# Four equal routing parts with one indirect zeroing transfer in the first expert layer, and re-dealt routing pieces ahead of the second

## The chip, the cores and the metric

The kernel runs on one core of a Trainium2 chip. The metric is the device time of one execution in microseconds (us). The engines are named as in the profile: PE (TensorE, the matrix unit; PEld is its weight load), DVE (VectorE), ACT (ScalarE), POOL (GpSimd) and SP (SyncE, which here only issues transfers). Each engine works through its own instructions in order and waits on semaphores for the others. A transfer is issued by SP, by ACT's queue or, where its addresses are computed row by row, by POOL as an indirect transfer. PSUM is the accumulator memory that PE writes into, in banks.

## The reference

The input is 2048 tokens (8 sequences of 256) of width 128, float32. Six residual steps follow one another:

```python
x = x + 0.5 * moe(layernorm(x))       # routed experts, first layer
x = x + attention(layernorm(x))       # 16 heads of width 8
x = x + 0.5 * moe(layernorm(x))       # the same weights, second layer
x = x + 0.5 * channel_mix(layernorm(x))
x = x + gated_conv(layernorm(x))      # a long convolution by Fourier transform
x = x + 0.5 * channel_mix(layernorm(x))

def moe(s):                           # 8 experts, each token goes to 2
    h = rmsnorm(s @ W_in.T, in_norm_w)
    logits = h @ Wr.T
    idx = top_k(logits + expert_bias, 2)
    g = softmax(logits at idx)
    for e in range(8):                # d_ff = 512
        oe = rmsnorm((silu(h @ Wg[e].T) * (h @ Wu[e].T)) @ Wd[e].T, enorm_w[e])
        out += (gate of e, 0 where it was not chosen) * oe
    return rmsnorm(out, out_norm_w) @ W_out.T
```

The kernel multiplies only the rows that were routed to an expert, so it has to sort 4096 (token, choice) rows by expert on the chip.

## The kernel before

**Layout.** The 2048 tokens are 16 tiles of 128, held in four chunks `xs[0..3]` of four tiles. The program order on PE, DVE, ACT and SP is written out by hand: whatever piece of the program is called first stands first in each engine's queue. POOL's routing transfers keep their program order too.

**Routing, `dispatch(f, i, parts, mp)`.** Layer `f` (0 or 1) is routed in parts; `parts[i]` names the first tile and the number of tiles. `EARLY` (L48) has five parts for layer one (2, 2, 4, 4 and 4 tiles), `LATE` (L49) five for layer two (4, 4, 4, 2, 2). A part is a list of pieces, called in this order, with the lines at which their instructions show in the profile:

- `turned`: PE transposes the tiles into the bank `pxt` (L337), ACT copies them out as `xnt` (L339).
- `product` twice, two tiles each: PE multiplies by the folded weights `win_r` (L359), ACT copies the result to `u` (L363) and sums its squares (L367).
- `measured`: DVE takes the mean and variance of the tiles (L347 to L351). Because of the layer norm the root of the mean square is corrected with `z`.
- `normed`: DVE forms `ri`, ACT takes its root (L377), DVE its reciprocal (L378). In the paced parts of layer two POOL takes the power instead.
- `logits` (DVE, L385) and `scaled` (ACT, L390), which writes the normalised rows into `hrow`, once for each of the two choices, with the token's number in column 128. A row has `ROW` = 129 words.
- `choice(0)` and `choice(1)` (DVE, L397 to L411): the best and the second best expert as one-hot vectors, and `mask`, their sum.
- `places`: the position of every row inside its expert's region. A triangular matrix `tri` times `mask` counts the earlier tokens of the tile (L418), one product with `ones` for each tile but the last adds the earlier tiles of the part (L420), one more product adds the earlier parts from `macc` (L427), and DVE extends `macc` by the part's counts `cnt` (L431, L432). DVE then forms `both`, `lsel`, `at_row`, `pos` and the integers `posi` (L434 to L445).
- `rows`: POOL writes each tile's 128 rows to their positions in the DRAM array `hs`, one indirect transfer for each tile and choice (L452), 32 in a layer.

`stagger(chunks, 4)` interleaves the parts of layer one: piece s - 4c of part c is called in step s, so a part starts four pieces after the one before it.

**The table.** Each expert has a region of `hs`. The experts read it in blocks of 256 or 128 rows whose last ones reach past the expert's count, so in layer one `zeros(first)` (L546) first writes 256 zero rows behind each expert's last row. It stands in `table` (L467), after the counts `pcnt` (L474), and `first` holds the eight start rows. Its core:

```python
for e in range(E):
    queue = (nc.sync, nc.scalar)[e % 2]
    row = nc.values_load(first[0:1, e : e + 1], engines=[queue.engine], ...)
    ins = queue.dma_start(hss[0][bass.ds(row, TT), :]..., zero)       # L553
```

The rest of `table` is a chain of small DVE operations (L476 to L543) that says for each block which expert it is and where it starts. For layer two the regions are cleared in advance, during the first expert stage, by `clear_rows` (`hs<-blank`, issued by SP).

**The experts.** `experts` takes 21 blocks in a fixed order (more if the table asks for them). SP reads an entry of the table into a register, fetches an expert's weights `w_f` (832 KB, L593) and a block of rows `hst_f` (L599); the first three blocks' fetches come ahead of everything, weights first in layer one, rows first in layer two. PE transposes the rows (`pht_f`, L605), multiplies gate and up (`pg_f`, `pu_f`, L615) and down (`py_f`, L638), and POOL scatters the results (L658).

**Around it.** The start of the program loads `x` and the constants, and folds the weights: DVE subtracts the mean (L294 to L298), PE transposes into `pwr` (L300), ACT copies it to `win_r` (L302). The fold stands ahead of all routing. `heads` (L810) holds the attention buffers; `qks[0]` and `qks[1]` are its 128 x 4096 word query and key buffers, first written during the expert stage.

**Layer two's routing** runs inside attention. Attention works in 34 numbered steps with places "a" and "b"; `at(step, place, *pieces)` hangs pieces there. Parts 0, 1 and 2 of `LATE` are spread over steps 12 to 33, and parts 3 and 4 stand in steps 32 to 34 with the end of the last sequence: `turn_back(7)`, `turn_heads(7)` and `out_heads(7)` turn the last averages `po` (L1014) into `x` (banks `pot`, `pcc`, `pwo`, and the addition L934). `keep_warm(out, n)` issues products of 128 columns whose result nobody reads. `root_table` makes ACT load the table of its root function ahead of need.

## Time and profile before

| what | value |
|---|---|
| median of 3 runs | 624.25 us (623.07, 624.25, 624.63) |
| profiled execution | 626.05 us, span 624.1 us, mean granted clock of PE 0.969 |
| busy over the span | PE 522.8 us (84%), DVE 356.1, ACT 271.0, POOL 192.1 |

Busy time of each engine by stretch of the span, in us, with the clock that PE was granted:

| stretch | what runs | PE | DVE | ACT | POOL | clock |
|---|---|---|---|---|---|---|
| 0 to 16.5 | loads, weight fold, first part's routing | 7.0 | 6.8 | 5.7 | 0.8 | 1.00 |
| 16.5 to 64.6 | routing of layer one, to POOL's last row | 16.3 | 27.5 | 18.8 | 30.9 | 1.00 |
| 64.6 to 75.4 | end of the table, first fetches | 0.7 | 3.1 | 0.0 | 0.0 | 1.00 |
| 75.4 to 185.6 | experts of layer one | 105.9 | 53.8 | 32.7 | 49.7 | 1.00 |
| 185.6 to 380.8 | combination, attention, most of layer two's routing | 177.9 | 133.6 | 112.5 | 38.2 | 0.99 |
| 380.8 to 411.8 | last of attention, rest of layer two's routing | 20.4 | 19.1 | 9.7 | 14.4 | 0.62 |
| 411.8 to 521.0 | experts of layer two | 103.1 | 43.8 | 30.5 | 35.4 | 0.98 |
| 521.0 to 624.1 | channel mixes and convolution | 91.5 | 68.6 | 61.0 | 22.7 | 0.96 |

Lines of the timeline read so: start in the span (us), duration (us), engine, line of the program, operation, output <- inputs, number of instructions drawn together, and in brackets how long the engine was idle before it and what ended that. SPq, ACTq and POOLq are those engines' transfer issues. The digits of the page's second part are tenths of busy time in 40 slices of 15.6 us each, and for PEclk tenths of full clock.

### The profile page before, as it was taken

What the parts mean: (1) busy time and instruction counts of PE and PEld (TensorE: products, weight loads), DVE (VectorE), ACT (ScalarE), POOL (GpSimd) and SP (SyncE); (2) the same over time, 40 slices, a digit from 0 to 9 for tenths busy, and PEclk for the clock granted to TensorE, in tenths of its full rate; (3) what the DMA queues carried; (4) which work ended last, traced back from release to release, by engine and by line L of the source; (5) the groups of instructions that cost most, each with busy time, mean ns of one, the idle gap of its engine ahead of it and who ended that gap; (6) DMA issues with size and microseconds to landing.
All of it is one profiled execution on the core that took longest, in us unless ns stands there. A gap on an engine that the chain in (4) does not pass through costs nothing.

```text
span 624.1 us, 11214 instructions
## 1 busy us (share of the span) xinstructions
PE 522.8 (84%) x3879; PEld 399.4 (64%) x3879; DVE 356.1 (57%) x1108; ACT 271.0 (43%) x662; POOL 192.1 (31%) x199
## 2 busy tenths in 40 slices
PE   4531299999989999899899987669999999889996
PEld 3521188898965555556556644449999984558884
DVE  3665255554443566767876884734444442777675
ACT  3532032222332455666765564213233232876265
POOL 0567135743343121001100446402333335520110
PEclk9999999999999999999999996599999998979999
DMA  6112647767723036408111001065778745000002
GB/s 224 35 38 94 202 154 211 207 194 219 218 79 102 27 43 174 168 35 257 51 49 22 26 26 51 31 217 178 216 222 252 216 137 147 1 0 2 2 1 67
DMA packets 38122, 71.70 MB, mean 115 GB/s; under 512 B 4587, under 2 KB 27922, under 8 KB 36912
## 3 DMA queue, kind: packets, MB, share of 16 engines
q1 hardware_dynamic: 33136, 61.97, 33.3%
q0 software_dynamic: 4352, 8.47, 3.9%
q8 instruction: 32, 0.52, 0.3%
q10 hardware_dynamic: 576, 0.53, 0.2%
q14 instruction: 26, 0.21, 0.1%
HBM read 50.10 MB, written 21.38 MB: 115 GB/s over the span
## 4 chain that ended last, share of the span: by engine, by line
PE 45%; ACT 9%; DVE 7%; DMA 5%; issue 3%; SPq 1%; POOL 0%; DVEq 0%; ACTq 0%; POOLq 0%
PE ps L967 8%; PE py_f L638 4%; PE pg_f L615 4%; PE pu_f L615 4%; ACT es L1004 4%; PE po L1014 4%; DMA y<-yrow_f,idx_f 3%; PE pvf L1343 2%; PE pgo L1370 2%; PE pm L950 1%; PE pk_m L1287 1%; DVE m L987 1%; PE pkv_m L1269 1%; PE pr_m L1269 1%; DMA w_f<-in_wall_dram 1%
## 5 line engine op out<-in xcount | busy, mean ns | idle before, releaser
L658 POOL DMA_INDIRECT y<-yrow_f,idx_f x72 | 70.7, 982 | 121.2 <-issue 61.8
L1004 ACT ACTIVATE es<-ps 128x1024 f32<-128x1024 f32 x64 | 65.3, 1020 | 51.7 <-PE ps L967 29.9
L987 DVE TENSOR_REDUCE m<-pm 128x4 f32<-128x1024 f32 x64 | 77.5, 1220 | 13.2 <-PE pm L950 13.1
L967 PE MATMUL ps<-qa,qk 32*128 32x256 f32 x512 | 72.8, 401 | 12.5 <-ACT es L1004 9.6
L452 POOL DMA_INDIRECT hs<-hrow,posi_f x64 | 61.7, 964 | 64.1 <-issue 28.7
L615 PE MATMUL pg_f<-ht_f,w_f 128*128 128x256 f32 (+1 forms) x336 | 71.5, 357 | 3.4 <-DMA w_f<-in_wall_dram 2.8
L638 PE MATMUL py_f<-w_f,hg_f 128*128 128x128 f32 x576 | 71.7, 276 | 2.4 <-issue 2.4
L950 PE MATMUL pm<-qk 32*128 32x256 f32 x512 | 73.1, 400 | 0.6 <-ACT qk L897 0.6
L638 PEld LDWEIGHTS py_f<-w_f,hg_f 128*128 128x128 f32 x576 | 69.5, 192 | 4.3 <-issue 2.7
L631 DVE TENSOR_TENSOR hg_f<-pu_f,sg_f 128x1024 f32<-128x1024 f32 (+1 forms) x42 | 45.0, 1071 | 43.4 <-PE pu_f L615 36.8
L615 PE MATMUL pu_f<-ht_f,w_f 128*128 128x256 f32 (+1 forms) x336 | 69.7, 350 | 0.0
L624 ACT ACTIVATE sg_f<-pg_f 128x1024 f32<-128x1024 f32 (+1 forms) x42 | 37.9, 901 | 59.5 <-PE pg_f L615 58.9
L967 PEld LDWEIGHTS ps<-qa,qk 32*128 32x128 f32 x512 | 43.6, 184 | 30.3 <-ACT es L1004 22.5
L648 ACT ACTIVATE ysq_f<-py_f 128x128 f32<-128x128 f32 x72 | 19.3, 273 | 99.6 <-PE py_f L638 92.1
L615 PEld LDWEIGHTS pg_f<-ht_f,w_f 128*128 128x128 f32 x336 | 56.1, 194 | 9.6 <-DVE hg_f L631 1.9
L615 PEld LDWEIGHTS pu_f<-ht_f,w_f 128*128 128x128 f32 x336 | 55.2, 192 | 5.6
L950 PEld LDWEIGHTS pm<-qk 32*128 32x128 f32 x512 | 44.2, 184 | 2.5 <-issue 1.5
L649 DVE TENSOR_TENSOR yrow_f<-py_f,w_f 128x256 f32<-128x256 f32 (+1 forms) x42 | 16.2, 387 | 45.0 <-ACT ysq_f L648 44.9
L607 DVE TENSOR_SCALAR ht_f<-pht_f,pack 128x256 f32<-128x256 f32 (+1 forms) x42 | 18.6, 444 | 33.5 <-PE pht_f L605 33.5
L605 PE MATMUL pht_f<-ident,hst_f 128*128 128x128 f32 x72 | 15.4, 283 | 24.5 <-DMA hst_f<-hs 24.5
L1014 PE MATMUL po<-es,v 128*32 128x256 f32 x512 | 35.7, 393 | 0.0
L161 POOL TENSOR_TENSOR cf_f<-cf_f,mhalf 128x8 f32<-128x8 f32 (+1 forms) x9 | 13.5, 1502 | 62.9 <-DVE cf_f L721 62.0
(271 smaller groups left out, 867.7 us busy)
## 6 DMA issues: line engine op xcount, KB each, us to landing
w_f<-in_wall_dram SPq DMA_DIRECT2D x41, 832.0 KB
hs<-blank SPq DMA_DIRECT2D x8, 1032.0 KB
hst_f<-hs SPq DMA_DIRECT2D x30, 129.0 KB
y_f<-y SPq DMA_DIRECT2D x14, 258.0 KB
pack<-in_pack_dram SPq DMA_DIRECT2D x1, 1729.0 KB
heads<-qkc SPq DMA_DIRECT2D x3, 512.0 KB
qk<-heads SPq DMA_DIRECT2D x12, 128.0 KB
y<-yrow_f,idx_f POOLq DMA_INDIRECT x72
```

The source lines that it names most:

```text
L452: ins = nc.gpsimd.indirect_dma_start(out=hss[f], out_offset=bass.IndirectOffsetOnAxis(ap=st["posi"][:, t, k : k + 1], axis=0), in_=hrow[:, ...
L615: nc.tensor.matmul(ph[:, k, :], w[t][:, o + k * P : o + k * P + P], ht[t], start=True, stop=True)
L624: nc.scalar.activation(sg, pg, AF.Silu)
L631: nc.vector.tensor_mul(hg[t], pu, sg)
L638: nc.tensor.matmul(py[:, s, :], hg[t][:, k, ts(s, P)], w[t][:, 2 * DFF + k * D : 2 * DFF + k * D + D], start=(k == 0), stop=(k == NFC - 1),)
L648: nc.scalar.activation(sq[:, s], py[:, s], AF.Square, accum_out=yrow[:, s, D : D + 1])
L658: ins = nc.gpsimd.indirect_dma_start(out=y2, out_offset=bass.IndirectOffsetOnAxis(ap=idx[:, s : s + 1], axis=0), in_=yrow[:, s, :], in_off ...
L950: nc.tensor.matmul(sc[:, jj, i, :], qs[c][r, g, col + i * P : col + (i + 1) * P], ks[c][r, g, col : col + S], start=True, stop=True,)
L967: nc.tensor.matmul(sc[:, jj, i, :], ks[c][r, g, col + i * P : col + (i + 1) * P], tops[s][r, :], start=True, stop=True,)
L987: nc.vector.tensor_reduce(m, sc, AX.X, ALU.max, negate=True)
L1004: nc.scalar.activation(es, sc, AF.Exp, scale=scale)
L1014: nc.tensor.matmul(po[32 * j : 32 * j + 32, :], vs[c][:, (b % 2) * 2 + i, (g % 2) * (H // 2) + (g // 2) * 4 + j, :], ess[s, j // 2][:, j % ...
```

## The change

**Layer one's parts.** `EARLY` becomes four parts of four tiles, one to each chunk. The list of pieces for the first part has `turned` and `measured` together, then the two products, an empty piece, and the rest; later parts have the order of before. In the first part `u` is copied out of PSUM by DVE instead of ACT, and ACT squares directly from PSUM.

**The ranks, both layers.** `macc` and `cnt` are replaced by `ahead`, one row of counts for each tile: DVE adds each tile's mask to the row before (one addition a tile), and PE needs two products in place of nt + 1, `tri` by `mask` and `ones` by the part's rows of `ahead`. `places` is split into `ranked` and `placed`, and `normed` into `summed` (with the root) and `inverted` (the reciprocal), so that other pieces can be called between the halves.

**The zeros.** `zeros` no longer loads registers. Constants say which expert a partition belongs to (`owner`, 16 partitions each) and where in the region its 16 rows start (`zrow`). Three DVE operations turn the counts into one word address for each partition, and one indirect transfer on POOL writes 16 rows of 129 words from each partition to that address. Its source `blank` is the first 2064 words of each partition of `qks[0]`, set to zero by DVE at the start; `heads` is therefore opened ahead of the routing. It is called with the counts in the last part, ahead of that part's rows; the program then places it on POOL between the first and the second of that part's eight row transfers. `table` gets the counts `pc` handed in.

**The fold** becomes a function `fold_in`, called after `heads` is opened, with nine filler products of `ident` by `ident` (128 columns each) ahead of `pwr`.

**Layer two.** The pieces of `LATE`'s parts 2, 3 and 4 in steps 31 to 34 are dealt out anew: the transposes and measures of part 3 move ahead of the last sequence's last weights, its products to step 33, the reciprocals and rank halves are called apart from the pieces they belonged to, and filler products `w(n)` in a bank of their own stand between them.

```diff
-EARLY = (0, 2), (2, 2), (4, 4), (8, 4), (12, 4)
+EARLY = (0, 4), (4, 4), (8, 4), (12, 4)
...
+    ahead = const.tile([P, NCH * TPC + 1, E], F32, tag="ahead", name="ahead")
+    nc.vector.memset(ahead[:, 0, :], 0.0)
...
             u = st["u"][:, 2 * i : 2 * i + 2]
-            nc.scalar.copy(u, pp)
+            first = f == 0 and t0 == 0
+            if first:
+                nc.vector.tensor_copy(u, pp)
+            else:
+                nc.scalar.copy(u, pp)
...
+                src = pp if first else u
                 nc.scalar.activation(
-                    sq[:, j], u[:, j, 0:D], AF.Square, accum_out=st["ss"][:, t : t + 1]
+                    sq[:, j], src[:, j, 0:D], AF.Square, accum_out=st["ss"][:, t : t + 1]
                 )
...
             nc.tensor.matmul(pr, tri, mask, start=True, stop=False)
-            for t in range(nt - 1):
-                nc.tensor.matmul(
-                    pr[:, t + 1 :, :],
-                    ones,
-                    mask[:, t : t + 1, :].to_broadcast([P, nt - 1 - t, E]),
-                    start=False,
-                    stop=False,
-                )
-            nc.tensor.matmul(
-                pr, ones, macc[:, i : i + 1, :].to_broadcast(sh), start=False, stop=True
-            )
-            cnt = small.tile([P, E], F32, tag="cnt", name=f"cnt_{n}")
-            nc.vector.tensor_reduce(cnt, mask.rearrange("p t e -> p e t"), AX.X, ALU.add)
-            nc.vector.tensor_add(macc[:, i + 1, :], macc[:, i, :], cnt)
+            for t in range(nt):
+                nc.vector.tensor_add(ahead[:, t0 + t + 1, :], ahead[:, t0 + t, :], mask[:, t, :])
+            nc.tensor.matmul(pr, ones, ahead[:, slots, :], start=False, stop=True)
...
+    def counts(f):
+        pc = bank(f"pcnt_{f}", "sb")[:, 0:E]
+        nc.tensor.matmul(pc, ones, ahead[:, NCH * TPC, :], start=True, stop=True)
+        return pc
+
+    def zeros(pc, mp):
+        at = mp.tile([P, E], F32, tag="zat", name="zat", bufs=1)
+        nc.vector.tensor_mul(at, pc, owner)
+        row = mp.tile([P, 1], F32, tag="zsum", name="zsum", bufs=1)
+        nc.vector.tensor_reduce(row, at, AX.X, ALU.add)
+        word = mp.tile([P, 1], I32, tag="zword", name="zword", bufs=1)
+        nc.vector.scalar_tensor_tensor(word, row, float(ROW), zrow, ALU.mult, ALU.add)
+        ins = nc.gpsimd.indirect_dma_start(
+            out=hss[0].rearrange("n w -> (n w)").unsqueeze(1),
+            out_offset=bass.IndirectOffsetOnAxis(ap=word, axis=0),
+            in_=blank[0],
+            in_offset=None,
+        )
...
-        for e in range(E):
-            queue = (nc.sync, nc.scalar)[e % 2]
-            row = nc.values_load(
-                first[0:1, e : e + 1], engines=[queue.engine], min_val=1, max_val=HS_ROWS - TT
-            )
-            ins = queue.dma_start(
-                hss[0][bass.ds(row, TT), :].rearrange("(p r) w -> p (r w)", p=P), zero
-            )
...
+        warm_i = bank("warm_i", "sb")
+        for i in range(9):
+            nc.tensor.matmul(warm_i[:, ts(i % 4, P)], ident, ident, start=True, stop=True)
...
+        blank.append(qks[0].rearrange("p i g s -> p (i g s)")[:, 0 : 16 * ROW])
+        nc.vector.memset(blank[0], 0.0)
...
         if f == 0:
-            return turned, *halves, measured, both(normed, logits, scaled), *choices, places, rows
-        return turned, *halves, measured, normed, logits, scaled, *choices, places, rows
+            start, places = both(summed, inverted, logits, scaled), both(ranked, placed)
+            if i == 0:
+                return both(turned, measured), *halves, lambda: None, start, *choices, places, rows
+            return turned, *halves, measured, start, *choices, places, rows
+        if i < len(parts) - 2:
+            return turned, *halves, measured, summed, logits, scaled, *choices, both(ranked, placed), rows
+        return turned, halves[0], measured, summed, inverted, logits, scaled, *choices, ranked, placed, rows
...
-                at(31, "a", partial(scaled, [2, 3]))
-                at(31, "b", choices[0])
+                at(31, "b", partial(scaled, [2, 3]), choices[0])
                 at(32, "a", choices[1])
-                at(32, "b", places, partial(rows, [0]))
-                at(33, "a", partial(rows, [1]))
-                at(33, "b", partial(rows, [2]))
...
-                at(32, "b", turned)
-                at(33, "a", half0, half1, measured)
-                at(33, "b", root_table, normed_)
-                at(
-                    34,
-                    "a",
-                    partial(turn_back, B - 1),
-                    rest,
-                    logits,
-                    choices[0],
-                    partial(turn_heads, B - 1),
-                    scaled,
-                    partial(out_heads, B - 1),
-                    t2,
-                    measured2,
-                    choices[1],
-                    h20,
-                    h21,
-                    places,
-                    rows,
-                    normed2,
-                    logits2,
-                    scaled2,
-                    *choices2,
-                    places2,
-                    rows2,
-                )
+                at(32, "a", w(3))
+                at(32, "b", x6, m6)
+                at(33, "a", u6, places, partial(rows, [0]))
+                at(33, "b", root_table, s6, partial(rows, [1]), w(2))
+                at(34, "a", partial(turn_back, b), partial(rows, [2]), w(4), i6, l6, c6[0])
+                at(34, "a", partial(turn_heads, b), partial(rows, [3]), w(2), h6, partial(out_heads, b))
+                at(34, "a", w(2), x7, w(2), m7, c6[1], u7, w(2), s7, r6)
+                at(34, "a", i7, p6, rows6, l7, *c7, h7, w(14), r7, p7, rows7)
...
-            stagger([dispatch(0, i, EARLY, gp) for i in range(len(EARLY))], 4)
...
             with tc.tile_pool(name="heads", bufs=1, reuse_waits="tile") as hp:
                 constant_pieces, attention = heads(hp)
+                fold_in()
+                parts = [[*dispatch(0, i, EARLY, gp)] for i in range(len(EARLY))]
+                found = {}
+
+                def counted():
+                    found["pc"] = counts(0)
+                    zeros(found["pc"], gp)
+
+                parts[-1][-1] = both(counted, parts[-1][-1])
+                stagger(parts, 4)
...
+        "owner": p // 16 == e[None, :],
+        "zrow": ROW * (REGION * (p // 16) + 1 + 16 * (p % 16)),
```

## The prediction

> **What bounds the kernel now.** I read the page first: PE is busy 84% of the span and carries 45% of the chain of waits, so the long stages (experts, attention, tail) belong to TensorE. The busy tenths show two holes in that row, slices 1 to 4 and slices 24 and 25, with the granted clock down in the second:
>
> ```profile
> PE   4531299999989999899899987669999999889996
> ...
> POOL 0567135743343121001100446402333335520110
> PEclk9999999999999999999999996599999998979999
> ```
>
> They are the two routing stages. The table of windows has PE busy 16.3 of 48.1 us in 16.5:64.6, and 20.4 of 31.0 us at a clock of 0.62 in 380.8:411.8, against 105.9 of 110.2 us in the expert stage between (75.4:185.6). What ends them is in the timelines. First layer:
>
> ```profile
> 16.67 1.17 POOL L452 DMA_INDIRECT hs<-hrow,posi_f  x1 [15.30 <-DVE z_f L351]
> ...
> 33.00 0.95 POOL L452 DMA_INDIRECT hs<-hrow,posi_f  x1 [4.58 <-issue]
> ...
> 44.56 0.95 POOL L452 DMA_INDIRECT hs<-hrow,posi_f  x1 [1.77 <-issue]
> ...
> 53.61 4.34 ACTq L553 DMA_DIRECT2D hs<-zero  x3
> ...
> 55.09 12.76 SPq L553 DMA_DIRECT2D hs<-zero  x4
> ...
> 63.57 0.96 POOL L452 DMA_INDIRECT hs<-hrow,posi_f  x1 [0.30 <-issue]
> 64.29 0.38 DVE L523 TENSOR_REDUCE tab_single<-tab_room 128x27 f32<-128x216 f32 x1 [3.12 <-issue]
> ...
> 68.64 0.36 SPq L593 DMA_DIRECT2D w_f<-in_wall_dram  x1
> ...
> 69.86 0.41 SPq L599 DMA_DIRECT2D hst_f<-hs  x1
> ...
> 74.11 0.69 PE L605 MATMUL pht_f<-ident,hst_f 128*128 128x128 f32 x2 [21.82 <-DMA hst_f<-hs]
> ```
>
> See three things. POOL's 32 row transfers run back to back at 1.267 us ((63.57 - 44.56) / 15) but stop before parts 1, 2 and 3. From 54 to 68 us, while SP and ACT issue the zeros, everything crawls: the table, 8.5 us in layer two (400.18 to 408.67), takes 17.0 us here (52.41 to 69.38), though its instructions are no longer. And SP, in order, starts weights and rows only after that; the rows then queue behind 832 KB of weights (4.2 us from issue to use; 2.3 us in layer two, 407.80 to 410.17).
>
> Second layer, from the last attention exponential on:
>
> ```profile
> 379.78 1.02 ACT L1004 ACTIVATE es<-ps 128x1024 f32<-128x1024 f32 x1 [0.76 <-PE ps L967]
> ...
> 380.26 2.52 PE L1014 MATMUL po<-es,v 128*32 128x256 f32 x16
> ...
> 388.46 0.42 DVE L934 TENSOR_TENSOR x<-pwo,x 128x256 f32<-128x256 f32 x1 [0.86 <-issue]
> ...
> 394.93 0.96 POOL L452 DMA_INDIRECT hs<-hrow,posi_f  x1 [5.53 <-ACT ri_f L377]
> ...
> 401.05 0.96 POOL L452 DMA_INDIRECT hs<-hrow,posi_f  x1 [1.37 <-issue]
> ...
> 404.83 0.96 POOL L452 DMA_INDIRECT hs<-hrow,posi_f  x1 [0.30 <-issue]
> ...
> 407.80 0.40 SPq L599 DMA_DIRECT2D hst_f<-hs  x1
> ```
>
> Here a serial chain runs on a cold PE (the average takes 2.52 us, 1.07 at 375.59), and POOL waits 5.53 and 1.37 us for positions.
>
> **What the Trainium skill says.** "TensorE: Matmul & The Clock Gate", Part 1: an idle PE runs at half rate, and some 3.4 us of sustained work bring it back. The trace agrees: eight gate halves take 3.75 us at 75.43 and 1.89 us at 81.38. "DMA: Bandwidth & Descriptors", Anatomy of one DMA (SWDGE): about 2 us are fixed, mostly the write's receipt. The trace has 1.4 us (scatter ended 187.02, dependent load issued 188.39) and at most 2.0 (405.79 to 407.80). The same page, "Why a DMA increments its semaphore by 16 and not by 1": one descriptor moves one contiguous run. No GpSimd transfer before the change has a long run, but the queue table counts 38122 - 36912 = 1210 packets of 8 KB or more: 58 instruction packets, 128 of the large constant pack and 8 x 128 of the SP-issued `hs<-blank`, whose rows are 16 x 516 = 8256 bytes, the length of the new zeros.
>
> **The change, part by part.** *Start.* The memset of 128x2064 replaces one of 128x258 (0.27 us). From 128x128 (0.17) and 128x258 the slope is 0.8 ns an element, so 1.7 us; one element a cycle would be 2.2. It runs from 1.2 to at most 3.5 us, before the constants (used at 4.27), so it costs nothing. Nine fillers ahead of `pwr`: a cold 128x136 product takes 0.545 us (2.18 / 4), so nine take up to 4.6 us from 1.45, and `pwr`, at 5.14 before, is late by 0 to 0.9; I take 0.5, after which PE is warm for part 0.
>
> *Part 0 with four tiles*: `pwr` to 6.3, copy 6.6, four transposes 7.35, copy (0.56) 7.95, four products (1.45 warm) 9.5. Each half then goes DVE copy (0.45), ACT squares (0.69): sums at 10.75. `ri`, root, reciprocal, logits as at 24.25: 0.9, to 11.65. The choices take 3.15 (25.19 to 28.07 and the logits' gap), to 14.8; four dependent additions (4 x 0.21) to 15.65. The rank product stands behind the next part's products (to 15.9) and ends at 16.6; places 0.9, to 17.5; POOL begins 0.8 to 1.2 later. I take **18.7** (18.0 to 20.0), against 16.67.
>
> *Every later part*: the rank loses three of five matmuls. At 28.07 the mask was ready and DVE resumed at 31.32, part of it behind products; after the change about 30.2. The part then repeats in 8.2 us instead of 9.34 (24.25 to 33.59), less than POOL's 8 x 1.267 = 10.1. So **POOL becomes the bound**, never waiting: 33 transfers (32 rows, 1 zeros) end at 18.7 + 33 x 1.267 - 0.3 = 60.2. The wait for the zeros' addresses hides: three small operations behind the count, ready about 43, POOL's turn at 51. Its bytes (1.06 MB; the page on DMA gives 6.15 us for 1 MB) lie beside seven more row issues, 8.9 us.
>
> *Zeros off SP and ACT*: eight issues and register loads leave. I take it that the crawl goes too. The table then runs from 43 to 53, SP issues the first weights at 54 and waits on the rows: at 60.2 + 1.4 = 61.6, with an empty queue, used 2.3 us later at **63.9 against 74.11: 10.2 us**. SP's second weights stand behind that wait as they do now, with the same spacing. The expert stage is PE's, so the shift is kept.
>
> *Second layer.* The last average now needs only the last exponential. Its transposes come before the last weights, so that exponential ends at 379.3 instead of 380.8, and warm (1.0) the average ends 380.5 (382.8). Warm `pot`, `pcc`, `pwo` (0.66, 0.38, 0.71 instead of 1.12, 0.66, 1.23), and no reciprocal waiting on a table load ahead of `rc`: x at 384.8 (388.88). The last part's logits come at 389.8 (394.69), its positions at 394.5 (400.27). The fillers fit in the copies' gaps. POOL again: part 2's rows start 381.2, then 16 x 1.267 without a stop end at 401.1 (405.79); the table's addresses come at 401.0 and SP takes 1.2. The row load moves from 407.80 to about 402.8: **5.0 us** (3.5 to 5.7). Should PE cool in the gap before the first gate, it costs little: PE waits 1.84 us for rows there anyway (415.63).
>
> *Attention*: two ranks lose 0.67 us of PE each (338.99 to 339.66), and DVE gains 0.84 - 0.29 us of additions each. Net 0.4 gained (-0.5 to +1.2).
>
> **Sum.** 10.2 + 5.0 + 0.4 = 15.6 us. The profiled execution took 626.05 us (span 624.1), so it would be 610.4; that execution is 1.8 above the median of 624.25, hence **608.7**.
>
> **Rivals.** *The crawl is not the zeros'* (15%). For: POOL's rows run through it too, and one DVE stall of 2.3 us (to 42.88) lies outside it. Against: register moves of SP and ACT take 0.69 us instead of 0.03 only there, and layer two's table, beside the same POOL rows, shows none of it. Then the table ends at 60, weights issue at 61.4, rows at 62.6 behind them, used at 66.8: 7.3 instead of 10.2, **611.6**.
>
> *The second layer gives little* (10%): positions come as late as now, because DVE, with longer additions, holds them up. Then at most 0.6 + 10.2: **613.5**.
>
> *Slower* (4%): the zeros' 2064 elements a partition, addressed by element, are cut into N pieces. POOL's price is 0.96 us for 128 descriptors, so 0.96 N us in order before seven row transfers. From N = 17 on the gain of 15.6 is gone; at single elements it is 0.96 x 2064 = 1981 us, about **2590**. Against: source and destination runs are contiguous, as are those of `hs<-blank`.
>
> **How the numbers follow.** Main case 70%: 605 to 612. A measurement of this kernel tells about 0.3% (1.9 us) from no change. All cases but the last are faster by more; 1% is left for a gain eaten elsewhere. Low end: 11.5 + 5.7 + 1.2 = 18.4 and a spread of 1 us, 604.5; high end: rival two with a later first row, 614.5.
>
> **What would show it.** Right: POOL rows without a stop from about 18.7 to 60, one `hs<-qk` of about 1 us among them; the table in about 9 us; weights issued before the rows; first expert transpose near 64; the second layer's row load near 403 with the clock of that window near 1. Wrong: POOL stopping between parts, a zeros transfer of many us, the table still 17 us, or the first rows' load waiting long after POOL's last operation.

## The result, and the profile after

The changed kernel took 617.56 us (median of 6 runs, 615.13 to 620.33), the kernel before 624.79 us beside it (6 runs, 623.07 to 626.06): a ratio of 0.9884 with a 95% interval of 0.9853 to 0.9914. It is faster, by 7.2 us. The prediction said faster, by 15.6 us, 608.7 us with a range of 604.5 to 614.5: the direction was right and the size was not; the measured time lies above the range. The profiled execution of the changed kernel took 619.62 us (span 617.8), against 626.05 us (span 624.1) before.

The busy tenths of the page, changed kernel:

```profile
PE   6401699999979999899899887869999989889996
...
POOL 0657056643332111102101346503333335510110
PEclk8555699999989999999999998889999998979999
```

In slices 24 and 25 PE is now at 7 and 8 instead of 7 and 6, with the clock at 8 and 8 instead of 6 and 5. The hole at the start, slices 1 to 4, holds as little as before: 5, 3, 1 and 2 tenths then, 4, 0, 1 and 6 now. (The clock digits of the first slices differ, 5 where 9 stood, but the eight product instructions of a part of four tiles take 2.18 us in both executions, at 18.76 before and at 12.70 after.) The timeline of the changed kernel, first layer:

```profile
17.48 1.17 POOL L461 DMA_INDIRECT hs<-hrow,posi_f  x1 [16.10 <-DVE amv_f L355]
...
30.42 0.19 DVE L419 TENSOR_TENSOR eq_f<-eq_f,pack 128x32 f32<-128x32 f32 x1 [1.00 <-DVE eq_f L418]
...
31.13 0.18 DVE L420 TENSOR_REDUCE mx_f<-eq_f 128x4 f32<-128x32 f32 x1 [0.52 <-DVE eq_f L419]
...
36.81 0.39 ACT L374 COPY u_f<-pin_f 128x272 f32<-128x272 f32 x1 [5.57 <-remote]
...
42.09 0.96 POOL L461 DMA_INDIRECT hs<-hrow,posi_f  x1 [4.46 <-issue]
...
53.47 0.96 POOL L495 DMA_INDIRECT hs<-qk,zword  x1 [0.30 <-issue]
...
59.13 0.00 SPq L612 DMA_DIRECT2D w_f<-in_wall_dram  x1
...
64.84 0.72 SPq L618 DMA_DIRECT2D hst_f<-hs  x1
...
67.06 0.69 PE L624 MATMUL pht_f<-ident,hst_f 128*128 128x128 f32 x2 [18.38 <-DMA hst_f<-hs]
```

The indirect zeros are one operation of 0.96 us, and the weights are issued ahead of the rows. But POOL stops once, for 4.46 us ahead of part 2 (42.09), because part 2's positions are late: from 28 to 40 us many of DVE's steps stand 0.71 us or more apart (30.42, 31.13) instead of 0.22, and ACT's copy waits 5.57 us for products that PE began at 28.82. Such a time, in which the small steps of several engines come far apart although each takes no longer, is called a slow stretch, or a stretch, below. Another one begins at 54 us and lies over the end of the table (the table runs from 49.32 to 63.10). So the crawl of the kernel before did not go with its zeros: it moved, and a second one came.

The second layer of the same execution:

```profile
372.15 1.02 ACT L1025 ACTIVATE es<-ps 128x1024 f32<-128x1024 f32 x1 [0.76 <-PE ps L988]
...
374.22 1.94 PE L1035 MATMUL po<-es,v 128*32 128x256 f32 x16
...
380.46 0.42 DVE L955 TENSOR_TENSOR x<-pwo,x 128x256 f32<-128x256 f32 x1
...
384.71 0.39 ACT L374 COPY u_f<-pin_f 128x272 f32<-128x272 f32 x1 [2.93 <-remote]
...
389.22 0.96 POOL L461 DMA_INDIRECT hs<-hrow,posi_f  x1 [3.40 <-issue]
...
400.89 0.40 SPq L618 DMA_DIRECT2D hst_f<-hs  x1
...
404.88 3.49 PE L634 MATMUL pg_f<-ht_f,w_f 128*128 128x256 f32 x8 [1.23 <-DMA w_f<-in_wall_dram]
```

Read against the first transpose of the first layer, the row load of layer two comes as late as it did: 400.89 - 67.06 = 333.83 us, and before 407.80 - 74.11 = 333.69. The 5.4 us that layer two and attention were to give are missing. The average starts 1.05 us after the last exponential has ended (374.22, against 373.17), ACT waits 2.93 us for products that PE began at 381.83, and POOL stops twice, for 3.37 us (to 376.00) and for 3.40 (to 389.22).

So the profiled gain of 6.3 us of span splits into 7.05 up to the first transpose, -0.14 from there to the row load of layer two, and -0.6 from there to the end. The forecast had 10.2, 5.4 and nothing. Of the 9.3 us that are missing, 3.15 lie ahead of the first transpose, 5.54 between it and the row load of layer two, and 0.6 behind.

### The profile page after: what moved, and what is told of

Read it like the earlier page. It is cut to its first block, busy times and chain, and to the rows that moved or that the text cites. A ratio compares the mean times of both kernels' runs of the same rounds, so it can differ in the third digit from the quotient of the medians.

```text
span 617.8 us, 11130 instructions
## 1 busy us (share of the span) xinstructions
PE 521.4 (84%) x3871; PEld 396.4 (64%) x3871; DVE 357.2 (58%) x1100; ACT 269.9 (44%) x658; POOL 193.6 (31%) x200
## 4 chain that ended last, share of the span: by engine, by line
PE 45%; ACT 9%; DVE 6%; DMA 5%; issue 3%; SPq 1%; POOL 0%; another core or an unknown queue 0%; ACTq 0%; DVEq 0%; POOLq 0%
PE ps L988 9%; PE py_f L657 4%; PE pg_f L634 4%; PE pu_f L634 4%; PE po L1035 4%; ACT es L1025 4%; DMA y<-yrow_f,idx_f 3%; PE pvf L1352 2%; PE pgo L1379 2%; DVE m L1008 2%; PE pm L971 1%; PE pk_m L1296 1%; PE pkv_m L1278 1%; PE pr_m L1278 1%; DMA w_f<-in_wall_dram 1%
## 5 line engine op out<-in xcount | busy, mean ns | idle before, releaser
L634 PE MATMUL pg_f<-ht_f,w_f 128*128 128x256 f32 (+1 forms) x336 | 73.0, 362 | 4.2 <-DMA w_f<-in_wall_dram 3.6
L643 ACT ACTIVATE sg_f<-pg_f 128x1024 f32<-128x1024 f32 (+1 forms) x42 | 37.9, 902 | 66.8 <-PE pg_f L634 66.1
L626 DVE TENSOR_SCALAR ht_f<-pht_f,pack 128x256 f32<-128x256 f32 (+1 forms) x42 | 18.7, 445 | 33.0 <-PE pht_f L624 33.0
```

What stands on the lines that cost most here:

```text
L634: nc.tensor.matmul(ph[:, k, :], w[t][:, o + k * P : o + k * P + P], ht[t], start=True, stop=True)
L643: nc.scalar.activation(sg, pg, AF.Silu)
```

## The experiments

Five groups of runs were made; kernels of one group ran on one chip beside the kernel before. The first group was a small kernel that tests the slow stretches by themselves; beside it the kernel before took 614.62 us in its single run, ten less than in the runs above, so the kernel before and the changed one were run again in the second group.

**A kernel of small steps (m1_steps).** Edit: the whole program replaced; GpSimd's part is `indirect_dma_start` of 128 rows in a loop, VectorE's a chain of `tensor_add(d, d, sync)`.

> Not the layer stack: the input is copied out, and between load and store six phases run one after the other. In each, VectorE works through a chain of dependent small additions (128x8, some 0.2 us a step), ScalarE and TensorE through small instructions of their own, while GpSimd sends indirect row transfers: (0) 24 of 128 rows of 516 bytes back to back, (1) none, (2) 24 with a pause of some 0.7 us after each, (3) 24 of 32 rows, (4) 24 of 128 rows of 64 bytes, (5) three runs of 8 with pauses of some 3 to 4 us. In the changed kernel the stretches in which every engine's steps take some 0.7 us or multiples of it begin at the ninth transfer of an unbroken run (27.81 in the first run, 53 us in the second) and end 1 to 3 us after the run. Theory A, a long unbroken run of row transfers slows the other engines: in phase 0 the additions go at 0.2 us for about 10.5 us, then at 0.7 us or more until some 3 us after the last transfer; phases 1, 2 and 5 stay at 0.2 us; phase 3 or 4 slows too if it is the number of transfers that counts, and stays clean if it is rows or bytes. Rival B, the slow stretches come with something else of the full kernel (instruction loads, which landed 0.5 to 1 us ahead of each of them, or register loads): the additions stay at 0.2 us in all six phases.

The phases ran into one another on GpSimd, which sent 57 transfers without a break from 6.81 on. The chain of additions beside them, in the table of windows of that tile (window, length, busy us and number of instructions, clock, DMA share, GB/s):

```profile
core 0: us, DVE busy (x), PEclk, DMA share, GB/s
...
17.00:36.00 19.00, 15.79 (x91) 1.00 0.17 52
```

91 steps in 19.0 us are 0.209 us each, past the ninth transfer as ahead of it. They ran beside the first 23 transfers and again from 77.36 us on, with the same step (60 in 12.59 us). A long run of transfers alone slowed nothing here; theory A as it was put fell.

**The kernel before and after once more, and two halves of the change undone (b1_before, a1_after, d1_deal_back, z1_zeros_back).** Edits: none in the first two; `d1_deal_back` has the `at(31..34)` lines of before, with

```diff
-        return turned, halves[0], measured, summed, inverted, logits, scaled, *choices, ranked, placed, rows
+        start = both(summed, inverted)
+        return turned, *halves, measured, start, logits, scaled, *choices, both(ranked, placed), rows
```

and `z1_zeros_back` has the `zeros(first)` of before in `table`, with `blank[0]` (258 words a partition) as the source.

> The kernel before, once more, for its trace beside the others of this group; in the single run beside the kernel of small steps it took 614.62 us, not 624. Theory A, the slow stretch of the first layer (every engine's steps at multiples of 0.7 us, 54 to 68 us in the first trace) comes and goes with the execution or the chip: if this one takes about 614, its table takes about 9 us instead of 17.0 and its first expert transpose stands near 66 instead of 74.11. Rival B, the stretch belongs to the kernel (its zeros' register loads): the table takes 17 us again, and a shorter time comes from somewhere else.

> The changed kernel once more. Theory A (slow stretches come and go): where they are absent, GpSimd has no stop of 4.46 us ahead of part 2, its last row ends near 59.5, the first transpose stands near 63, and the gain over the kernel before shrinks to 3 to 5 us, since that one loses its slow stretch too. Rival B: first transpose at 67 as before, gain 7 us.

> The changed kernel with the second layer's pieces dealt as before (new ranks, zeros and first layer kept). The prediction: 5.0 us slower than the changed kernel (3.5 to 5.7). Theory A, from the traces: from the first transpose of layer one to the row load of layer two it was 333.69 us before and 333.84 after, so the dealing is worth nothing there and this kernel equals the changed one within 1 us. Rival C: the dealing does gain some 2 to 3 us and a stall of ScalarE of 2.1 us (382.5 to 384.7) hid it in that execution; then this one is 2 to 3 us slower.

> The changed kernel with the zeros as before: eight transfers on SP's and ScalarE's queues with addresses from registers (source: 258 zeroed words of the same buffer). Theory A (the slow stretches are not the zeros'): one transfer less on GpSimd (1.27 us), but four issues ahead of SP's first weights; 0 to 3 us slower than the changed kernel. The prediction's own view (the zeros' register loads make the slow stretch): a table of 17 us and 7 to 10 us slower.

| group 2 | median us | ratio to before (95%) |
|---|---|---|
| before, 14 runs | 617.75 (616.48 to 624.19) | |
| b1_before, one run | 618.35 | |
| a1_after | 610.46 | 0.9845 (0.9802 to 0.9888) |
| d1_deal_back | 612.91 | 0.9900 (0.9862 to 0.9938) |
| z1_zeros_back | 609.21 | 0.9827 (0.9785 to 0.9869) |

Timeline of the kernel before in b1_before:

```profile
51.47 3.79 SPq L553 DMA_DIRECT2D hs<-zero  x4
...
57.21 0.37 SPq L593 DMA_DIRECT2D w_f<-in_wall_dram  x1
...
67.12 0.69 PE L605 MATMUL pht_f<-ident,hst_f 128*128 128x128 f32 x2 [17.13 <-DMA hst_f<-hs]
```

The same program, the same zeros, and no crawl: four zeros are issued in 3.79 us instead of 12.76, the table takes 8.4 us (50.22 to 58.64) instead of 17.0, and the first transpose stands at 67.12 instead of 74.11. Of the 14 runs of before in this group five took 620.87 to 624.19, the others 616.48 to 619.82. And the changed kernel beside it, a1_after, both layers:

```profile
62.42 0.69 PE L624 MATMUL pht_f<-ident,hst_f 128*128 128x128 f32 x2 [22.57 <-DMA hst_f<-hs]
...
372.78 0.42 DVE L955 TENSOR_TENSOR x<-pwo,x 128x256 f32<-128x256 f32 x1
...
377.52 0.17 DVE L400 TENSOR_TENSOR lg_f<-u_f,ri_f 128x16 f32<-128x16 f32 x1
...
390.84 0.40 SPq L618 DMA_DIRECT2D hst_f<-hs  x1
...
394.88 3.75 PE L634 MATMUL pg_f<-ht_f,w_f 128*128 128x256 f32 x8 [1.19 <-DMA w_f<-in_wall_dram]
```

This is the timeline that the prediction drew. POOL does not stop from 17.28 to 58.84, the table takes 8.4 us (40.49 to 48.91), the last logits come 4.74 us after `x`, POOL's 16 rows of layer two follow one another from 369.38. The gain of 8.5 us of span against b1_before is 4.70 up to the first transpose, 6.21 from there to the row load of layer two (334.63 - 328.42), and -2.4 after it.

Theory A held and rival B fell: the stretch is not in every execution of the kernel before. The gain of 3 to 5 us that theory A gave for the whole was too little; by the medians it was 7.3. Undoing the dealing cost 2.45 us by the medians, 5.4 at the row load of layer two (333.82 - 328.42), so rival C is right. Putting the zeros back on the queues was expected to be 0 to 3 us slower and was not: it was 1.25 us faster by the medians, with runs that overlap (608.65 to 610.79, and 608.60 to 611.89), and 0.6 at the first transpose (61.81), in one trace of each. Its table took 8.7 us (40.33 to 49.01), so the register loads alone do not make a stretch. Without stretches the indirect transfer gains nothing that shows, and as one more transfer on the engine that binds it may cost a little.

**Smaller edits (r1_rank_first, w1_warm_more, t1_three, o1_only_four).**

```diff
-                at(33, "a", u6, places, partial(rows, [0]))
+                at(33, "a", places, u6, partial(rows, [0]))      # r1, t1, c1
...
-                keep_warm(bank("warm_t", "pz"), 34)
+                keep_warm(bank("warm_t", "pz"), 56)               # w1, t1, c1, w2
...
-EARLY = (0, 2), (2, 2), (4, 4), (8, 4), (12, 4)
+EARLY = (0, 4), (4, 4), (8, 4), (12, 4)                           # o1: this alone, on the kernel before
```

`t1_three` also has the zeros of z1_zeros_back. `o1_only_four` has a `macc` of six rows so that layer two still fits.

> The changed kernel with one swap in step 33: part 2's rank products stand ahead of part 3's products instead of behind them. In the trace of a1_after the rank waits until 367.04 for ScalarE's copy of part 3's product (both use one PSUM bank, and the copy stands behind the last exponential), the last average waits behind the rank, and GpSimd stops for 3.23 us (to 369.38). Theory A (this order costs): rank at about 365.6, GpSimd's stop shrinks to about 1.7 us, the average starts with the end of the last exponential (0.8 us earlier), row load of layer two 1.2 us earlier (the table's addresses bind next, at about 389.6); 0 to 1.2 us faster in all, less if TensorE cools as before. Rival B (the stop is hidden): no difference.

> The changed kernel with 56 instead of 34 filler products between the last rank and the first expert transpose of layer two. In a1_after TensorE idles 4.54 us there and the first gate takes 3.75 us, against 0.78 us and 1.96 us in b1_before; from first transpose to third gate block it is 9.49 us against 7.99. The prediction: cooling there costs little, since TensorE waits for rows anyway; under 0.3 us of difference. Theory A: the cold gate is on the path; gate at about 2.0 us, 1.5 us faster in all (1.0 to 1.8).

> Three edits at once on the changed kernel: zeros by eight queue transfers as before, the rank ahead of part 3's products, 56 fillers. If they add up: 1.2 (measured as 610.46 against 609.21 in the group before) + 1.2 + 1.5 = about 3.5 us faster than the changed kernel; if the row load is bound by the table's addresses and the weights anyway: 1.5 to 2.5.

> The kernel before with nothing but the four equal parts in layer one (old ranks, zeros, second layer). Theory A (the parts are what layer one gains, since a part of four tiles repeats in 9.34 us and GpSimd needs 10.14 us for its rows): GpSimd starts near 19 and never stops, ends near 59.5 to 60, first transpose near 63.5 against 67.12; 3 to 4 us faster than before, half of the whole change. Rival B (the shorter ranks and the early fold are needed): stops stay, under 1.5 us faster.

| group 3 | median us | ratio to before (95%) |
|---|---|---|
| before, 43 runs | 624.22 (622.61 to 630.25) | |
| r1_rank_first | 618.81 | 0.9891 (0.9855 to 0.9927) |
| w1_warm_more | 617.48 | 0.9899 (0.9850 to 0.9948) |
| t1_three | 623.00 | 0.9971 (0.9955 to 0.9987) |
| o1_only_four | 625.68 | 1.0020 (0.9998 to 1.0042) |

The changed kernel did not run in this group. All four traces show the stretches, and the expectations, made without them, missed. w1_warm_more, at 617.48, is where the changed kernel was in its other groups with stretches (616.50 to 618.24), so the 1.5 us expected of a warm gate do not show. With the four parts alone POOL starts at 19.90, stops for 4.49 us ahead of part 2 (44.50) and the table takes 17.5 us (52.36 to 69.81): no gain. In `r1_rank_first` the swap did what it should (POOL's first stop 1.70 us, the average warm at 372.89), and then ACT's copy of part 4's products waited 3.92 us and POOL 5.39 ahead of part 3's rows. It looks as if the run of rows that now began earlier met a stretch earlier. The issues of `t1_three`:

```profile
52.23 13.23 SPq L493 DMA_DIRECT2D hs<-qk  x4
...
71.52 0.69 PE L622 MATMUL pht_f<-ident,hst_f 128*128 128x128 f32 x2 [22.66 <-DMA hst_f<-hs]
```

In a stretch the queue's zeros do cost what the prediction took from the trace: SP spends 13.23 us on four of them (4.08 us in z1_zeros_back) and the first transpose comes at 71.52, against 66.84 and 67.15 in r1 and w1, which have the indirect zeros. So beside stretches 4.4 to 4.7 us of the first layer's gain come from taking the zeros off the queues; how the rest divides among parts, ranks and fold was not tested.

**What sets a stretch off (p1_pause, m2_steps), with two for comparison (c1_rank_warm, a2_after).** Edits: `p1_pause` puts three memsets of `ms[0]` on GpSimd ahead of part 1's rows,

```diff
         def rows(ts_=range(nt)):
+            if f == 0 and i == 1:
+                for _ in range(3):
+                    tc.keep_in_program_order(nc.gpsimd.memset(idle_[0], 0.0))
```

and `m2_steps` makes each phase of the small kernel wait for the one before it.

> The changed kernel with one pause of some 3 us on GpSimd (three memsets of an unused buffer) between the eighth and the ninth row transfer of layer one. Where slow stretches occur, they ran from 28.2 to 40.4 us (the ninth transfer of the first run starts at 27.81) and from about 54 us (the ninth to tenth of the second run, which starts at 42.09). Theory A (nine or more row transfers without a break set it off): with the pause the second run starts near 31, no slow step between 28 and 40, part 2's positions come by 33 to 34 and GpSimd does not stop ahead of part 2; the slow stretch comes from about 41.5 on instead; first transpose within 1 us of the changed kernel's. Rival B (it comes at its own time, whatever GpSimd does): slow steps from 28 us all the same, and a first transpose 3 us later. If this chip shows no stretch in the changed kernel either: GpSimd just ends 3 us later, first transpose 3 us later, and nothing is decided.

> The kernel of small steps again (the input is copied out), now with the six phases kept apart: 24 row transfers of 128 rows of 516 bytes back to back, none, 24 with a pause of 0.7 us after each, 24 of 32 rows, 24 of 128 rows of 64 bytes, three runs of 8 with pauses of 4 us; VectorE's dependent additions beside them, 0.21 us each in m1_steps. Told by the times of the kernel before in this group whether the chip is one with slow stretches (about 624) or not (about 615 to 618). Theory A on a chip with stretches: additions at 0.7 us from the ninth transfer of phase 0 on, none in phases 1, 2 and 5; rival B: none in any phase. On a chip without: none in any phase under both.

> The changed kernel with part 2's rank ahead of part 3's products and 56 fillers (the indirect zeros kept). On a chip without stretches: 1.2 + 1.5 = up to 2.7 us faster than the changed kernel, at least the 1.5 of the warm gate; on one with stretches: row load of layer two as late as in the changed kernel, so only the 0.5 to 1.5 of the warm gate.

> The changed kernel, for comparison in this group: 7 us faster than the kernel before on either kind of chip, by layer one where there are slow stretches (first transpose near 67 against 74) and by layer two where there are none.

Medians: before 624.14 (23 runs), p1_pause 617.87 (ratio 0.9892, 0.9859 to 0.9925), c1_rank_warm 619.00 (0.9924, 0.9896 to 0.9952), a2_after 616.50 (0.9872, 0.9830 to 0.9915). This chip had the stretches. The timeline of p1_pause:

```profile
27.39 2.98 POOL L459 MEMSET m<- 128x1024 f32 x3
...
30.54 0.96 POOL L464 DMA_INDIRECT hs<-hrow,posi_f  x1 [0.16 <-ACT u_f L374]
...
44.15 0.28 DVE L529 TENSOR_REDUCE tab_cum<-tab_over 128x16 f32<-128x128 f32 x1 [1.20 <-issue]
```

With a pause of 3.15 us after the eighth transfer the additions and comparisons from 28 to 40 us are a normal 0.22 us apart, part 3's positions come by 40.3 us, and POOL does not stop again. The stretch starts at 42.7 instead, 12 us after the second run's first transfer, and lies over the table. The first transpose, at 67.41, is no later for the pause than in the changed kernel (67.06 in the first profile, 68.43 in a2_after). So the pause moved the stretch; by the medians it made nothing faster. c1_rank_warm was not faster but 2.5 us slower than a2_after. As in r1, part 2's rows started sooner and POOL then stopped for 5.35 us ahead of part 3, so nothing was gained at the row load of layer two (332.79 us after the first transpose, 332.35 in a2_after). The loss itself lies behind it in the two traces (217.7 us to the end against 213.5) and is not assigned. The windows of the chain of additions in m2_steps: phase 0 up to its onset and from it on, all of phase 2, phases 3 and 4 from their onsets on:

```profile
core 0: us, DVE busy (x), PEclk, DMA share, GB/s
6.70:16.90 10.20, 8.11 (x47) 1.00 0.15 47
16.90:41.10 24.20, 4.39 (x26) 1.00 0.14 46
75.00:118.30 43.30, 36.02 (x215) 1.00 0.11 36
...
130.40:156.50 26.10, 3.67 (x21) 1.00 0.05 11
...
185.60:211.00 25.40, 4.31 (x25) 1.00 0.03 6
```

Length by number gives a step: 0.217 us at first, 0.93 from about the eighth transfer on (16.9, the run began at 6.99), 0.20 where each transfer is followed by a pause of 0.70 us. Transfers of 32 rows (0.87 us on GpSimd instead of 0.96) and rows of 64 bytes set it off as well, 7.7 and 8.4 us into their runs, with steps of 1.24 and 1.02 us. In three runs of 8 with pauses the steps are slow only from 242.06 to 244.9 and from 255.5 to 258.4, at the end of the first two, where theory A had none. ACT's and PE's steps slow at the same moments; GpSimd goes on at its own pace. So rows and bytes are not what sets a stretch off here, but a run without a break: some seven transfers in phases 3 and 4, eight in phase 0, ten in p1_pause. Number and time (7.7 to 12 us) cannot be told apart, since all unbroken runs here were spaced 1.17 to 1.27 us. Something else has to hold besides: m1_steps sent the same first 24 transfers on another chip, a1_after is the changed kernel itself, and neither has a stretch.

**The last group (a3_after, d2_deal_back, w2_warm_more, f1_five).** `f1_five` is the changed kernel with the five-part `EARLY` of before.

> The changed kernel for comparison in this group, 7 to 8 us faster than the kernel before on either kind of chip.

> The second layer dealt as before, all else changed. If this chip has the slow stretches: the new dealing makes GpSimd's rows one unbroken run, which sets off a stretch in layer two (a2_after: 7.4 us from x at 380.19 to the last logits at 388.19, against 6 us before), so the dealing is worth 0 to 1 us there. If it has none: 2.4 us slower than the changed kernel, as in the first group.

> The changed kernel with 56 instead of 34 fillers ahead of layer two's first transpose. Without slow stretches: the gate takes 2.0 instead of 3.75 us and the kernel is 1.0 to 1.8 us faster; the prediction had put this cooling at about nothing. With them: TensorE idles less there anyway (a2_after's gate took 1.97 us), 0 to 1 us.

> The changed kernel with the five parts of before in layer one (2, 2, 4, 4, 4 tiles), all else kept. Without slow stretches: GpSimd starts earlier (about 15.5) but stops for some 2 us after the first part and 3 us after the second; its last row 1 to 2 us later than in the changed kernel (58.84), so 1 to 2 us slower. With them: [...] the stretch ahead of part 3 may not come at all; between 2 us faster and 2 us slower.

| group 5 | median us | ratio to before (95%) |
|---|---|---|
| before, 43 runs | 625.25 (622.29 to 631.37) | |
| a3_after | 618.24 | 0.9884 (0.9829 to 0.9939) |
| d2_deal_back | 622.49 | 0.9949 (0.9926 to 0.9971) |
| w2_warm_more | 618.77 | 0.9888 (0.9831 to 0.9944) |
| f1_five | 623.02 | 0.9957 (0.9937 to 0.9977) |

This was the chip of group 2 again, and now every trace had the stretches: the condition changes on one chip. The dealing is worth 4.25 us by the medians, more than was expected beside stretches; at the row load it is 2.84 (335.51 after the first transpose, 332.67 with the dealing). The traces alone do not show it, since five with the new dealing and stretches (the first profile, a2, a3, w1 and w2) lie between 332.35 and 336.26 there. More fillers made no difference, the gate being warm already in a3_after (1.97 us). In `f1_five` the stops of 1.63 and 3.29 us after the first parts did not, as was hoped, keep the stretch away: the run that begins with part 2 at 29.96 has slow steps from 39.9, and POOL stops 4.57 us later (48.89 to 54.4) instead of earlier. By the medians five parts are 4.8 us slower than four. The two traces show only part of it: 0.76 us at the first transpose (69.51 against 68.75) and 1.4 in the whole execution (620.34 against 618.96).

No version beat the changed kernel clearly: z1_zeros_back was 1.25 us faster by the medians, within the spread of the runs, where there were no stretches, and t1_three, with the same zeros, 4.2 to 5.5 us slower than its neighbours r1 and w1 where there were.

## Why the prediction missed

**The zeros and the crawl: the step that failed.** "I take it that the crawl goes too" is the step behind the 10.2 us of the first layer. The forecast set a kernel before with a stretch (first transpose 74.11) against a kernel after without one (63.9). No run made that pair. With stretches on both sides it was 7.05 us (74.11 to 67.06), without them 4.70 (67.12 to 62.42; the drawn 63.9 was even 1.5 late). The evidence against it was named in the prediction: rows that ran through the crawl, and a DVE stall outside it. It was outweighed by a coincidence of place: the register moves took 0.69 us because they stood in a slow stretch, not the other way round, and layer two's clean table stood beside runs of only four row transfers (broken at 389.4 and 399.7), where layer one's stands beside one of sixteen. The first rival, "the crawl is not the zeros'", is what the first layer did: first transpose forecast at 66.8, measured 67.06. That the number fits so well is luck. The rival had the table end at 60 and the rows behind the weights; here the weights were out at 59.13, and the rows waited for a table that ended at 63.10 and for POOL's last row, which ended at 63.46.

**POOL never waiting.** Right in a1_after (no stop, last row 58.84 against a forecast 60.2, with a start at 17.28 instead of 18.7). In the profiled run above POOL's unbroken run met a stretch. By the forecast's sum it would have ended at 17.48 + 33 x 1.267 - 0.3 = 58.99; it ended at 63.46. The stop of 4.46 us, 4.16 more than the usual 0.30 between two transfers, is the term that the forecast put at nothing.

**Zeros as one transfer of 0.96 us.** Size right (0.96 at 53.47; the rival of many pieces fell), and its place as the 33rd transfer of the run was counted. Its worth shows only beside a stretch, where SP spends 13.23 us on the zeros otherwise.

**Start.** The memset (1.78 us, 1.7 forecast) and the fillers (`pwr` at 5.32 against 5.14 before, 0.5 late forecast, 0 to 0.9) are right. The first row came 1.2 us early (17.48), and most of that arose ahead of the squares: the copy of the folded weights ended at 6.03 (6.6 worked out), the four products at 8.60 (9.5), the last sum at 9.80 (10.75).

**Second layer, 5.0 us: the larger miss beside stretches.** Right where no stretch lies: 6.21 us with attention's share, against 5.0 + 0.4. There `x` to logits is 4.74 us (5.0 forecast) and the average warm. One term was mis-sized: the average was to end 1.2 us after the last exponential and ended 1.97 after it (366.70 to 368.67), because part 2's rank stands ahead of it and waits for ACT's copy of part 3's products; r1_rank_first removes that wait. In the profiled run above the gain was lost, and the step that failed is "16 x 1.267 without a stop": the run of 16 rows was broken for 3.40 us, ahead of 389.22, after ACT had waited 2.93 us for part 4's products. Set beside a1_after, the row load comes 5.41 us later after the first transpose. Of these, 2.37 lie between `x` and the row load, with that stop, 1.21 between the last exponential and `x`, with an average of 1.94 us on a PE at a clock of 0.59 (374 to 378 us), and 1.83 ahead of the end of that exponential, which no run assigns. That is the second rival in size, by another cause than the one it named. An unbroken run of rows is what the forecast counted on, and what p1_pause and m2_steps show to set a stretch off; that the 2.93 us wait is such a stretch is read from its look, the run before it having had seven transfers only.

**Cooling ahead of the first gate "costs little".** The gate took 3.75 us in a1_after, after 4.54 us of idle, and 1.96 in b1_before after 0.78; that agrees with the Trainium skill, "TensorE: Matmul & The Clock Gate", Part 1, on an idle PE's half rate. And from the first transpose of layer two to the gate of the second block it was 9.49 against 7.99 us, 1.5 more. Beside stretches it goes by the idle time too: 3.49 us after 3.64 of idle in the first profile, 1.97 in a2_after and a3_after after 1.03 and 1.17. In the medians the 1.5 us could not be shown: w1 and w2, whose gates took 1.99 us, only ran beside stretches, and w2 was no faster than a3_after. From the row load of layer two to the end the profiled runs of all kernels vary from 213.5 to 218.1 us, so the -2.4 of a1_after is not assigned.

**The range.** The two rivals were given 15% and 10% as if one excluded the other. Both happened at once in the profiled run: 624.25 - 7.3 - 0.6 = 616.4, near the measured 617.56 and outside the range. They seem to have one cause, the stretches, and a range made of single cases leaves that out. In neither condition was the gain near 15.6 us: by the medians it was 7.2, 7.6 and 7.0 beside stretches and 7.3 without. That these agree is chance, since the gain lies in the first layer with stretches and in both layers without. Two sums of the prediction are a little off, and neither matters here: the low end should read 604.85 (624.25 - 18.4 - 1), and attention's terms, two ranks at 0.67 - 0.55, come to 0.24 if simply taken together, and not 0.4.

## What to carry to other kernels

A stretch in which every engine's steps take the same odd time is first to be looked for in a second execution of the same kernel, before an edit is credited with removing it; here one trace had 17.0 us for a table that took 8.4 in another. Where it returns, count what ran without a break ahead of it: here seven to ten indirect transfers. A pause after eight moved the stretch and did not make the kernel faster (617.87 against 616.50); fewer transfers were not tried. And when two rivals can share a cause, the range has to hold them together.

## What was not expected of the hardware

Back-to-back indirect transfers from GpSimd can slow the small steps of DVE, ACT and PE, DVE's from some 0.2 to 0.93 us and more (m2_steps), beginning 8 to 12 us into the run and ending some 4 us after it (41.1, where the last transfer ended at 37.1; 6 us in phase 3), without GpSimd itself slowing. The steps do not take longer, they stand further apart. Spaced at 1.83 us instead of 1.267 the transfers slowed nothing in the same execution. On other occasions runs as long slowed nothing either (57 transfers in m1_steps, 33 in a1_after), and one chip was seen both ways (a1_after and a3_after). What differs then, and what the engines share, stays open; nor does any run show whether the recording of the trace takes part in it.

A transfer's time on GpSimd hardly depends on its size: 0.96 us for 128 rows of 516 bytes, of 64 bytes, or of 8256 bytes, and 0.87 us for 32 rows.
